# Two graph-attention layers: the first graph's lists made beside layer 0, and another order of steps in layer 1

## The chip, the core and the metric

One core of a Trainium2 chip runs the whole program. The metric is the device time of one execution in microseconds; lower is better. The core has five engines with a queue each: PE (matrix multiply, with its weight loads as PEld), DVE (vector), ACT (activation), POOL (which here also issues the gathers) and SP (which here issues most transfers). Each queue is worked off in order; engines wait for each other by semaphores.

## What is computed

There are 16 graphs of 1024 nodes with 256 features, and a dense 0/1 matrix `adj` for each. Layer 0 and layer 1 are attention layers, each followed by a residual sum and a layer norm:

```python
# layer 0, all graphs together where _bn takes its means
Wh = einsum('bnf,of->bno', x, W)
att = (Wh @ a1)[:, :, None] + (Wh @ a2)[:, None, :]
att = softmax(_bn(leaky(_bn(att, g1, b1)), g2, b2), axis=2) * adj
x = layernorm(x + elu(_bn(einsum('bij,bjo->bio', att, Wh), g3, b3)))
# layer 1, per head of 4
fts = x @ W[h]
logits = (fts @ w1[h])[:, :, None] + (fts @ w2[h])[:, None, :]
coefs = 0.5 * softmax(leaky(logits) - 1e9 * (1 - adj)) + 0.5 * softmax(adj)
x = layernorm(x + mean_h(elu(coefs @ fts + x)))
```

`_bn` in layer 0 takes the mean and variance over all graphs, so the last step of layer 0 (the factors `s3`, `t3` of the third `_bn`) can only be taken when the aggregation of all 16 graphs is finished, and layer 1 can only start from it. `adj` has few ones: layer 1 works on lists of neighbours.

## The kernel before

**Layer 0** (line 200 on). A first stage loads x, forms `wh` and casts `adj` to 16 bit; a second finds the statistics of the first two norms. The aggregation (L607 to L631) then runs over the 16 graphs. For graph b it makes 16 steps n; a step is `aggregate` (L568, four matmuls on PE), and at even n also `weights` (L525) for the graph after. After the last graph, `store` and L633 to L645 give `s3` and `t3`; L1023 makes `t31`. Outside the block that is marked as ordered by hand, the order in each engine's queue is set at build time by a scheduler that goes by the order in the text and by what is ready.

**Between the layers** (L1025 to L1135). Some hundred small DVE instructions make constants: the matrix `IW` by which h is turned, `MX`, the bit values `bits` and `add16`, `cols`, `lanes` and others. Among them are a load of one row of W, spread over all partitions (`wl`, L1120, 512 KB), and its subtraction from `W1s` (L1122).

**Lists** (class `Lists`, L1138). For each graph, lists of the columns that its groups of rows use:
- `load_rows` (L1147) loads the 16-bit adjacency in two halves of 1 MB; `words` (L1156, 32 matmuls a half) packs the bits of 25 rows into words; `worded` copies them (ACT, L1167) and sums the rest (DVE, L1171).
- `used`, then `places` (ten matmuls, L1183 to L1186) numbers the columns that are used; `placed` (L1195 to L1201) takes the number apart.
- `low`, `high`, `higher` build one-hot tables on DVE; `pick` (L1259, 64 matmuls) brings the columns into their places; `picked`, `order` (L1290) and `indices` (L1297) give `ix`, the row numbers for the gathers.

**Nodes** (class `Graph`, L1386). For each graph `load_h` (L1398) loads what layer 0 left, `exps` (ACT, L1418 and L1421) and `elu` (DVE, L1428) apply the elu in four pieces, `turn` (PE, L1434) turns it, `residual` and `beside` (DVE) add x and keep the logits, `means` and `squares` (ACT) and `spans` and `norm` take the layer norm, `factors`, `raised` and `scale` (ACT, L1481) apply it, `table` (L1508) stores the rows to memory. `halve`, `total` and `store_total` (L1530) add the sum over all rows.

**Gathers and units** (classes `Chunk` and `Unit`, L1321 and L1580). `fetch` (POOL, L1338) gathers rows by `ix`; `weigh` (DVE, and one copy on ACT at L1360) makes their weights. A graph has 16 units, two for each group of 125 + 3 rows. A unit's path: `gather` (PE, L1550, into a PSUM pair of three buffers), `invert` (DVE, L1608), `norm` (ACT, L1616, which frees the pair), `turn` and `turned` (L1622, L1632), `linear` (L1642), `add` (DVE, L1650), `exps` (L1656), `sum`, `squares`, `mean`, `span`, `power`, `close`, `store`.

**Order.** The loop at L1817 walks n from -30 to the last unit, each unit one step. The text inside the loop is the order of the queues: it is ordered by hand. `stand(part, n)` calls the side work that `side` (L1739) has filed: part 0 before the exps, 1 between the gathers on PE, 2 (loads, exps, squares, scale, fetches) and 3 (weigh). The tables `AT`, `FETCH` and `WEIGH` say at which n, counted from the graph's first unit, each step is filed. A graph's side work begins 29 units ahead, so it runs beside the two graphs before it; for the first graph there is nothing to run beside. Steps of a later graph come first in a call.

Turns and list steps share two PSUM buffers (`ps_s`).

Of the kernel before, what the change touches and what calls it, by code (L numbers as in the profile page):

```python
# [12 lines left out]
I32 = mybir.dt.int32  # L13
# [14 lines left out]
def kernel(  # L28
# [170 lines left out]

    with ExitStack() as l0:  # L200
# [17 lines left out]
        with tc.tile_pool(name="apool", bufs=1) as apool, tc.tile_pool(  # L218
# [86 lines left out]
            mts = {b: mask(mpool, b, "mt0") for b in range(min(2, B))}  # L305

# [210 lines left out]
        with tc.tile_pool(name="wk", bufs=1) as wk, tc.tile_pool(  # L517
# [47 lines left out]

            acc = {}
# [40 lines left out]
            for b in range(B):  # L607
                for n in range(NH * K):
# [416 lines left out]
    with ExitStack() as l1:  # L1025
        xpool = l1.enter_context(tc.tile_pool(name="x1pool", bufs=3))
        hpool = l1.enter_context(tc.tile_pool(name="hpool", bufs=1))
# [5 lines left out]


        TW = P + 2 * H
        IW = pk.tile([P, C, TW], F32, name="IW")
        for oc in range(C):
            nc.vector.tensor_copy(IW[:, oc, 0:P], ident)
        nc.vector.tensor_copy(IW[:, :, P:TW], WW)

        QR = (H + 1) * QB
        MX = pk.tile([P, H, QB], F32, name="MX")
        MY = pk.tile([P, H, QB], F32, name="MY")
        nc.vector.tensor_tensor(
            MX, ident[:, 0 : H * QB].rearrange("p (h q) -> p h q", h=H),
            al_bc.unsqueeze(2).to_broadcast([P, H, QB]), ALU.mult,
        )
        nc.vector.tensor_tensor(  # L1050
            MY, ident[:, H * QB : QR].unsqueeze(1).to_broadcast([P, H, QB]),
            om_bc.unsqueeze(2).to_broadcast([P, H, QB]), ALU.mult,
        )
        nc.vector.tensor_tensor(MX, MX, MY, ALU.add)

        bits = pk.tile([P, QB], F32, name="bits")
        for i in range(QB):
            nc.vector.memset(bits[:, i : i + 1], float(1 << i))  # L1060
        ibits = pk.tile([P, QB], I32, name="ibits")
        nc.vector.tensor_copy(ibits, bits)
        nc.vector.memset(bits[:, QB - 1 : QB], -float(1 << (QB - 1)))

        every = pk.tile([P, 1], I32, name="every")
        nc.vector.memset(every, (1 << QB) - 1)

        add = pk.tile([P, K, NB + 1], F32, name="add")
        pick = pk.tile([P, NB, QB], F32, name="pick")
        nc.vector.tensor_tensor(  # L1070
            pick, ident[:, 0 : NB * QB].rearrange("p (n q) -> p n q", n=NB),
            bits.unsqueeze(1).to_broadcast([P, NB, QB]), ALU.mult,
        )
        nc.vector.tensor_reduce(add[:, 0, 0:NB], pick, AX.X, ALU.add)
        nc.vector.tensor_copy(
            add[:, 1:K, 0:NB], add[:, 0, 0:NB].unsqueeze(1).to_broadcast([P, K - 1, NB])
        )
        last = pk.tile([P, K, 3], F32, name="last")
        nc.vector.tensor_tensor(
            last, ident[:, NB * QB : P].unsqueeze(1).to_broadcast([P, K, 3]),  # L1080
            bits[:, 0 : 3 * K].rearrange("p (k q) -> p k q", q=3), ALU.mult,
        )
        nc.vector.tensor_reduce(add[:, :, NB], last, AX.X, ALU.add)
        add16 = pk.tile([P, K, NB + 1], BF16, name="add16")
        nc.vector.tensor_copy(add16, add)


        cols = pk.tile([P, K, NQ], FP16, name="cols")
        jj = pk.tile([P, K, NQ], I32, tag="pi", name="jj", bufs=1)
        nc.gpsimd.iota(jj, pattern=[[P, K], [0, NQ]], base=-N, channel_multiplier=1)  # L1090
        nc.vector.tensor_copy(cols, jj)
        in8 = pk.tile([P, 8], F32, name="in8")
        nc.vector.tensor_reduce(in8, ident.rearrange("p (r q) -> p q r", q=8), AX.X, ALU.add)
        in8h = pk.tile([P, 8], FP16, name="in8h")
        nc.vector.tensor_copy(in8h, in8)
        in16 = pk.tile([P, 16], F32, name="in16")
        nc.vector.tensor_reduce(in16, ident.rearrange("p (r q) -> p r q", q=8), AX.X, ALU.add)
        in16h = pk.tile([P, 16], FP16, name="in16h")
        nc.vector.tensor_copy(in16h, in16)
        far = pk.tile([P, 24], FP16, name="far")  # L1100
        for i in range(24):
            nc.vector.memset(far[:, i : i + 1], float(2048 + P + 16 * i))


        rows = pk.tile([P, 9, 8], F32, name="rows")
        nc.vector.memset(rows, float(N))
        nc.vector.memset(rows[0:1, 0:NB, :], float(N + 1))
        nc.vector.memset(rows[0:1, 6, 0:1], float(N + 1))

        low = pk.tile([P, K, 48], FP16, name="low")  # L1110
        nc.vector.memset(low, 99.0)
        act = pk.tile([P, K + 1, NQ], BF16, name="act")
        nc.vector.memset(act, 0.0)
        lanes = pk.tile([P, 16, 8], FP16, name="lanes")
        for i in range(16):
            nc.vector.memset(lanes[:, i], float(i))


        wl = pk.tile([P, H, F], F32, tag="rw", name="wl", bufs=2)
        nc.sync.dma_start(wl, W[:, F - 1, :].partition_broadcast(P))  # L1120
        for fc in range(C):
            nc.vector.tensor_tensor(W1s[:, fc], W1s[:, fc], wl, ALU.subtract)  # L1122
# [764 lines left out]
```

The softmax here doesn't subtract the row's maximum and nothing guards it: scores larger than these inputs give would overflow.

## Time and profile before

| what | us |
|---|---|
| median of 3 runs (2366.23 to 2368.56) | 2366.42 |
| the profiled execution | 2364.92 |
| its span | 2363.2 |
| first stage and casts | 0 to 185 |
| statistics of layer 0 | 185 to 298.8 |
| aggregation of layer 0 | 298.8 to 796 |
| from there to dense work in layer 1 | 797 to 893 |
| layer 1 | 893 to the end |
| PE, DVE, ACT, POOL busy in the whole span | 2105.5, 1916.6, 1435.5, 1060.5 |

Times in the trace count from the span's start. A line of a timeline gives the start, the duration, the engine, the line of the kernel, the operation with output and inputs, the shapes, the number of instructions, and in brackets the idle time of the engine before it with what ended it. PE's clock is given as a share of full speed.

### The profile page before, as it was taken

The numbers are of one execution on the slowest core, as the hardware profiler recorded it, in microseconds if no ns is written. First come the engines' busy times: TensorE is split into PE (matmuls) and PEld (weight loads), VectorE is DVE, ScalarE is ACT, GpSimd is POOL, SyncE is SP. The second block draws the span as 40 slices with busy tenths as digits, with TensorE's granted clock in tenths as the row PEclk, the third lists the DMA queues.
The fourth block names the chain that finished last, engine by engine and source line by source line (L and its number), as shares of the span: only waits on it lengthen the run. The fifth ranks groups of instructions, "written<-read, shape, count | busy, mean of one in ns | idle before, by whom it ended". The sixth has DMA issues, their size and how long they took to land. (4 is left out here: it accounts for less than half of the span.)

```text
span 2363.2 us, 36997 instructions
## 1 busy us (share of the span) xinstructions
PE 2105.5 (89%) x12503; PEld 1647.8 (70%) x12503; DVE 1916.6 (81%) x4800; ACT 1435.5 (61%) x3028; POOL 1060.5 (45%) x1133
## 2 busy tenths in 40 slices
PE   6992479999999549899999999999999999999997
PEld 5772434444444338788888888788888788887886
DVE  3334899999999357888988989888889789898886
ACT  1122777777777226567676675675676666756665
POOL 0000100000000036776767766767767667667682
PEclk9995589999999758899999999999999999999999
DMA  8969959985553348576675685675666756756651
GB/s 258 285 191 236 263 115 244 226 206 154 155 155 93 116 147 215 160 179 174 171 196 177 157 213 162 161 206 160 181 176 172 198 162 163 210 166 164 138 149 52
DMA packets 342359, 419.75 MB, mean 178 GB/s; under 512 B 172760, under 2 KB 273168, under 8 KB 336016
## 3 DMA queue, kind: packets, MB, share of 16 engines
q1 hardware_dynamic: 285840, 256.24, 36.7%
q0 software_dynamic: 55104, 158.54, 30.4%
q10 hardware_dynamic: 1216, 2.51, 0.3%
q8 instruction: 101, 1.65, 0.3%
q14 instruction: 98, 0.80, 0.1%
HBM read 346.47 MB, written 104.29 MB: 191 GB/s over the span
## 5 line engine op out<-in xcount | busy, mean ns | idle before, releaser
L1338 POOL DMA_INDIRECT xc<-xe_dram,ix x640 | 690.7, 1079 | 184.8 <-issue 166.3
L1642 PE MATMUL pv<-W1s,sT 128*128 128x256 f32 x2048 | 504.6, 390 | 0.3 <-ACT sT L1636 0.3
L572 PE MATMUL pa<-em,wh 128*128 128x512 f32 x1024 | 451.3, 599 | 17.8 <-DVE em L536 13.4
L1642 PEld LDWEIGHTS pv<-W1s,sT 128*128 128x128 f32 x2048 | 381.6, 197 | 44.0 <-ACT sT L1636 0.7
L1622 PEld LDWEIGHTS pt<-MX,s 125*128 125x128 f32 x2560 | 355.3, 206 | 31.0 <-ACT sT L1632 9.1
L572 PEld LDWEIGHTS pa<-em,wh 128*128 128x128 f32 x1024 | 193.9, 192 | 250.4 <-issue 237.3
L1550 PE MATMUL pu<-xc,w 128*125 128x256 f32 x1280 | 365.4, 401 | 0.0
L1622 PE MATMUL pt<-MX,s 125*128 125x100 f32 x2560 | 355.6, 289 | 4.8 <-ACT sT L1632 2.9
L1656 ACT ACTIVATE m<-v,neg 128x512 f32<-128x512 f32 x256 | 184.1, 719 | 251.0 <-DVE v L1650 199.6
L1616 ACT ACTIVATE s<-pu,z 125x256 f32<-125x256 f32 x640 | 260.6, 472 | 113.3 <-DVE z L1608 63.3
L1550 PEld LDWEIGHTS pu<-xc,w 128*125 128x125 f32 x1280 | 238.6, 197 | 37.5 <-issue 6.1
L528 ACT ACTIVATE e<-eb,c,s 128x1024 f32<-128x1024 f32 x128 | 155.0, 1236 | 79.0 <-DVE sm L542 42.6
L1632 ACT COPY sT<-pt 128x500 f32<-128x500 f32 x256 | 147.1, 575 | 91.7 <-PE pt L1622 91.6
L1650 DVE TENSOR_TENSOR v<-pv,x 128x512 f32<-128x512 f32 x256 | 175.0, 683 | 8.2 <-PE pv L1642 7.9
L532 ACT ACTIVATE e<-e,v,u 128x1024 f32<-128x1024 f32 x128 | 152.3, 1229 | 22.7 <-DVE e L531 16.6
L1699 POOL TENSOR_TENSOR ors<-ors,mhalf 128x1 f32<-128x1 f32 x128 | 97.7, 764 | 149.2 <-DVE ors L1693 147.6
L536 DVE TENSOR_TENSOR em<-e,mt 128x1024 f32<-128x1024 f32 x128 | 155.6, 1218 | 3.4 <-PE pa L572 2.1
L1434 PE MATMUL pz<-IW,h 128*128 128x136 f32 x512 | 96.4, 324 | 68.1 <-DVE hi L1200 29.8
L531 DVE SCALAR_TENSOR_TENSOR e<-e 128x1024 f32<-128x1024 f32 x128 | 151.4, 1216 | 0.0
L1434 PEld LDWEIGHTS pz<-IW,h 128*128 128x128 f32 x512 | 81.7, 217 | 84.7 <-issue 46.2
L147 POOL TENSOR_TENSOR s<-var,mhalf 128x2 f32<-128x2 f32 x1 | 0.7, 710 | 311.9 <-DVE var L146 311.9
L293 DVE COPY wx<-pw 128x266 f32<-128x266 f32 x128 | 55.3, 434 | 98.3 <-PE pw L289 98.3
(320 smaller groups left out, 3558.8 us busy)
## 6 DMA issues: line engine op xcount, KB each, us to landing
x<-in_x_dram SPq DMA_DIRECT2D x32, 1024.0 KB
adj<-in_adj_dram POOLq DMA_DIRECT2D x16, 2048.0 KB
rw<-adj SPq DMA_DIRECT2D x32, 1024.0 KB
A<-u_dram SPq DMA_DIRECT2D x128, 250.0 KB
wh_dram<-wx SPq DMA_DIRECT2D x16, 1024.0 KB
wh<-wh_dram SPq DMA_DIRECT2D x16, 1024.0 KB
h_dram<-hb SPq DMA_DIRECT2D x16, 1024.0 KB
h<-h_dram SPq DMA_DIRECT2D x16, 1024.0 KB
```

Source lines behind the costliest of these rows:

```text
L528: nc.scalar.activation(e, ebs[b], AF.Identity, bias=c1[:, k, b : b + 1], scale=s1[:, k : k + 1])
L532: nc.scalar.activation(e, e, AF.Exp, bias=v2[:, k : k + 1], scale=u2[:, k : k + 1])
L536: nc.vector.tensor_tensor(em, e, mts[b][:, k, :], ALU.mult)
L572: nc.tensor.matmul(acc[b, hf, oc], wh[b][:, k, oc * P : (oc + 1) * P], ems[b, k][:, hf * HALF : (hf + 1) * HALF], start=(k == 0), stop=(k ...
L1338: nc.gpsimd.indirect_dma_start(out=self.xc[:, i, :], out_offset=None, in_=xe_dram[g.b % 2], in_offset=bass.IndirectOffsetOnAxis(ap=g.l.ix[ ...
L1434: nc.tensor.matmul(pz[:, oc, :], self.h[:, oc, k * P : (k + 1) * P], IW[:, oc, :], start=True, stop=True,)
L1550: nc.tensor.matmul(pu[0:QR, 0:F], c.w[:, k].rearrange("p h q -> p (h q)"), c.xc[:, k, 0:F], start=(i == 0), stop=(i == len(OF[q]) - 1),)
L1616: nc.scalar.mul(f.s[0:QR, i], f.pu[i][0:QR, 0:F], f.z[0:QR, i : i + 1])
L1622: nc.tensor.matmul(self.pt[:, i].rearrange("p h q -> p (h q)"), self.first.s[0:QR, i, self.hp * P : (self.hp + 1) * P], MX[0:QR].rearrange ...
L1642: nc.tensor.matmul(self.pv[:, hh, :], self.first.sT[:, fc, self.hp * HP + hh, :], W1s[:, fc, self.hp * HP + hh, :], start=(fc == 0), stop= ...
L1650: nc.vector.tensor_tensor(self.v2, self.pv, self.g.x[:, self.it].unsqueeze(1).to_broadcast([P, HP, F]), ALU.add)
L1656: nc.scalar.activation(self.m, self.v2, AF.Exp, bias=neg1, scale=1.0)
```

## The change

Four things are done.

1. The constants move from between the layers to a place in layer 0's block, right after the first stage; they lie in a pool of their own (`ek`). The pool `hpool` moves out too: it holds in turn `jj`, `wl` and `h0`, the h of graph 0.
2. The lists of graph 0 are made in the aggregation of the last graph of layer 0. Their tiles borrow buffers of layer 0 (`room`). The rows are loaded in the aggregation of the graph before, h of graph 0 at its step 4.
3. The side work of graph 0 has no lists; its x is loaded at step -29 instead of -23, and the rows of graph 1 right behind. Some numbers in the tables change.
4. In the loop over units, the steps stand in another order.

```diff
+    m1 = ExitStack()
+    ek = m1.enter_context(tc.tile_pool(name="ek", bufs=1))
+    hpool = m1.enter_context(tc.tile_pool(name="hpool", bufs=1))
...
             mts = {b: mask(mpool, b, "mt0") for b in range(min(2, B))}
+        TW = P + 2 * H
+        IW = ek.tile([P, C, TW], F32, name="IW")
...
+        wl = hpool.tile([P, H, F], F32, tag="h", name="wl")
+        nc.sync.dma_start(wl, W[:, F - 1, :].partition_broadcast(P))
+        for fc in range(C):
+            nc.vector.tensor_tensor(W1s[:, fc], W1s[:, fc], wl, ALU.subtract)
+        nc.sync.dma_start(W1s[P - 1 : P, C - 1], bias1[0:1])
...
+        h0 = hpool.tile([P, C, N], F32, tag="h", name="h_0")
...
+            def half(self, shape, dtype, name, hf):
+                if not self.room:
+                    return pk.tile(shape, dtype, tag="rw", name=f"{name}_{self.b}_{hf}", bufs=2)
+                if hf == 0:
+                    self.both = mpool.tile([P, 2 * shape[1], *shape[2:]], dtype, tag="mt", name=f"{name}_{self.b}")
+                return self.both[:, hf * shape[1] : (hf + 1) * shape[1]]
...
+        lists0 = Lists(0)
...
+            lists0.room = dict(
+                wl=(ek, "wl", 1), ix=(ek, "ix", 1), hA=(epool, "wh", 2),
+                pi=(wk, "e", 4), hi=(wk, "e", 4), hA1=(wk, "e", 4), hA2=(wk, "e", 4),
+                hm=(wk, "em", 11), V=(wk, "em", 11), E=(wk, "em", 11),
+            )
+            def make_lists(n):
+                s = lists0
+                steps = {
+                    0: [lambda: s.words(0)],
+                    1: [lambda: s.worded(0), lambda: s.words(1)],
+                    2: [lambda: s.worded(1), s.used],
+                    3: [s.places],
+                    4: [s.placed, lambda: s.high(0)],
+                    5: [lambda: s.low(0), lambda: s.low(1)],
+                    6: [lambda: s.low(2), lambda: s.low(3)],
+                    7: [lambda: s.high(1), s.higher],
+                    11: [s.pick],
+                    12: [s.picked],
+                    14: [s.order],
+                    15: [s.indices],
+                }
+                for step in steps.get(n, ()):
+                    step()
...
+                    if n == 4 and b == B - 1:
+                        nc.sync.dma_start(h0, h_dram[0])
+                    if b == B - 2 and n == 1:
+                        for hh in range(NH):
+                            lists0.load_rows(hh)
+                    if b == B - 1:
+                        make_lists(n)
...
         AT = {
-            'lh': -29, ('rw', 0): -29, ('rw', 1): -28, ('words', 0): -27, ('words', 1):
+            'lh': -29, ('rw', 0): -29, ('rw', 1): -29, ('words', 0): -28, ('words', 1):
...
-            'mean': (-17, -14), 'elu': (-26, -25, -24, -23), 'turn': (-22, -21, -19,
+            'mean': (-17, -14), 'elu': (-28, -25, -24, -23), 'turn': (-22, -21, -19,
...
         FETCH = {
-            'l': (-7,), 0: (-7, -6, -6, -6, -6), 'm': (-6, -6, -5, -5, -4), 'n': (-4,
-            -4), 1: (-4, -3, -3, -3, -3), 'o': (-2, -2), 2: (-1, -1, 0, 0, 0), 3: (1, 1,
-            1, 1, 2), 4: (2, 3, 3, 3, 3), 5: (3, 4, 4, 4, 5), 6: (5, 5, 6, 6, 7), 7: (7,
+            'l': (-7,), 0: (-7, -6, -6, -6, -6), 'm': (-6, -6, -5, -4, -4), 'n': (-4,
+            -4), 1: (-3, -3, -3, -3, -3), 'o': (-2, -2), 2: (-1, 0, 0, 0, 0), 3: (0, 1,
+            1, 1, 2), 4: (3, 3, 3, 3, 3), 5: (4, 4, 4, 4, 5), 6: (5, 5, 6, 6, 7), 7: (7,
...
         WEIGH = {
-            'l': -5, 0: -3, 'm': -2, 'n': -1, 1: 0, 'o': 0, 2: 2, 3: 4, 4: 6, 5: 8, 6:
+            'l': -5, 0: -3, 'm': -2, 'n': -1, 1: 0, 'o': 1, 2: 2, 3: 4, 4: 6, 5: 8, 6:
...
+            if g.b == 0:
+                after[AT["lh"]] += [g.load_x]
+                if B > 1:
+                    for hf in range(2):
+                        after[AT["lh"]] += [each(graphs[1].l.load_rows, hf)]
+            else:
+                after[AT["lx"]] += [g.load_x]
+            if g.b:
+                for hf in range(2):
+                    if g.b > 1:
+                        after[AT["rw", hf]] += [each(lists.load_rows, hf)]
+                    turned(AT["words", hf], lists.words, lists.worded, hf)
...
             for n in range(-EARLY, len(units) + 12):
+                do(n - 6, "add")
                 do(n - 9, "power")
-                do(n - 6, "add")
                 stand(0, n)
                 do(n - 6, "exps")
                 do(n - 3, "turn", "turned")
+                stand(2, n)
+                do(n - 7, "mean")
+                do(n - 8, "span")
+                do(n - 10, "close")
+                do(n - 5, "linear")
                 do(n - 1, "invert")
+                do(n - 11, "store")
                 do(n - 1, "norm")
-                stand(2, n)
-                do(n - 10, "close")
-                do(n - 11, "store")
-                do(n - 5, "linear")
                 if 0 <= n < len(units):
                     units[n].gather(0)
                 stand(1, n)
-                if 0 <= n < len(units):
-                    units[n].gather(1)
-                do(n - 7, "mean")
-                do(n - 8, "span")
                 stand(3, n)
                 do(n - 6, "sum")
                 do(n - 7, "squares")
+                if 0 <= n < len(units):
+                    units[n].gather(1)
```

In the queues this order means: on ACT a unit's `norm` stands behind part 2 of the side work and behind `close`; on DVE `mean` and `span` stand ahead of `invert`; on PE, POOL and SP the order of these steps is the same.

More of the change, by code (lines that the diff above doesn't have):

```diff
@@ L1050 @@
[L1050 to L1077, printed above, removed]
@@ L1098 @@
[L1098 to L1110, printed above, removed]
@@ L1750, in side @@
             after[AT["lh"]] += [g.load_h]
[L1751 to L1762 removed]
+            if g.b == 0:
[3 more added lines that the diff above has]
+                        after[AT["lh"]] += [each(graphs[1].l.load_rows, hf)]
+            else:
+                after[AT["lx"]] += [g.load_x]
[4 more added lines that the diff above has]
+                    turned(AT["words", hf], lists.words, lists.worded, hf)
+                early[AT["used"]] += [lists.used]
+                turned(AT["places"], lists.places, lists.placed)
+                for part in range(4):
+                    early[AT["low"][part]] += [each(lists.low, part)]
+                for part in range(2):
+                    early[AT["high"][part]] += [each(lists.high, part)]
+                early[AT["higher"]] += [lists.higher]
+                turned(AT["pick"], lists.pick, lists.picked)
+                turned(AT["order"], lists.order, lists.indices)
             for n in range(2 * C):
```

434 lines of the change are left out of this document (226 added, 208 removed).

## Prediction

> **What bounds the kernel now.** I read the page's slices first, then the busy time by stage, then the timelines of the passage from layer 0 to layer 1 and of one ordinary graph, then the waits of the steady stretch. (The page's chain of the last work only names the very end and is of no use here.) By stage, with the columns PE, PEld, DVE, ACT, POOL busy, clock, DMA share, GB/s:
>
> ```profile
> 770.00:797.00 27.00, 26.22 (x79) 12.79 (x78) 4.53 (x16) 4.00 (x10) 0.00 (x0) 1.00 0.18 74
> 797.00:893.00 96.00, 37.64 (x296) 28.61 (x297) 55.39 (x255) 28.00 (x66) 24.54 (x25) 0.55 0.49 150
> 893.00:2206.00 1313.00, 1244.32 (x8186) 1095.19 (x8186) 1134.88 (x3252) 859.29 (x2190) 916.33 (x947) 0.94 0.67 178
> ```
>
> In the last aggregation (770 to 797) PE is full and DVE has 22.5 us free. Then 96 us pass in which no engine is full: a chain of dependent steps. From 893 on PE is 95% busy and DVE 86%. The passage, one line each from the timelines of ACT, PE, DVE and SP:
>
> ```profile
> 798.60 0.18 ACT L594 ACTIVATION_READ_ACCUMULATOR dist<-hb,mn 128x1 f32 x1
> 812.49 0.30 ACT L1167 CAST fw<-pc 128x160 int32<-128x160 f32 x1 [13.70 <-PE pc L1156]
> ...
> 838.22 6.03 PE L1259 MATMUL po<-hA,B 128*128 128x64 f16 x64 [2.50 <-DVE fs L1451]
> ...
> 844.29 0.56 DVE L1269 TENSOR_TENSOR ptt<-po,in 128x384 f32<-128x384 f32 x1 [5.59 <-PE po L1259]
> ...
> 854.76 0.37 SPq L1508 DMA_DIRECT2D xe_dram<-x  x1
> ```
>
> Layer 0 is finished when L1023 ends at 801.8. The first exp of graph 0 needs only that and h, yet it stands behind fw on ACT, so behind the words, the constants and the load of wl: 812.7. Later `spans` (L1468) stands on DVE behind `picked` until 847.3, though its squares were done at 841.3. The node table of graph 0 is stored at 854.76, 53.0 us after 801.8; the gathers start 10.1 us later.
>
> **Part 1, lists of graph 0 and constants leave the passage: -24.9.** I rebuild it from t = 0 at 801.8, every duration from the rows of that stretch. ACT: four exp pairs, 1.55 each as at 812.7 to 819.0, so elu is done at 5.5 for the third piece and 7.1 for the fourth. PE: the eight turns need the third piece for k below 4; at the half clock of this stretch (0.50 at 815 to 820) one takes 1.1, so 5.6 to 14.4. x no longer holds residual: its load moves from step -23 to -29, and its 8.2 us (814.1 to 822.3) start, even if queued behind the last store of h, before t = 0. Residual and fs of the eighth end at 15.0, its four squares (2.5) at 17.9, spans and the power on POOL (1.9 as at 847.3) at 19.9.
>
> Here a **new wait** comes in. `elu` of graph 1 moved from -26 to -28, so graph 1's first exp pair stands on ACT ahead of graph 0's `raised` and `scale`, and its elu stands on DVE ahead of `norm` and `factors`. It needs h of graph 1, whose load waits for the eighth turn (as at 835.75) and takes 5.1: 19.6. The pair ends at 21.4, fw copy and elu at 22.6, factors (1.07) at 23.7, raised and scale (0.37 and 4.02) at 28.1. Table at 28.1 instead of 53.0: **24.9 saved**. Without that wait it would be about 2 more (27); if h of graph 1 takes the 8.2 that x took, 3 less (22). The two loads of rows of graph 1 (1 MB each) now precede h on SP; two took about 10 us at 844 to 854, and they have 14. Their words therefore don't wait as at 849.7. From table to the first gathers nothing of the chain is changed (halves, total, xr), so I keep the 10.1.
>
> **Part 2, the lists go where PE is full: +11.5.** Words 2 x 0.9, places 1.1, pick 5.9, order 0.3 as at 1511 and 1549: 9.2 of PE behind which the aggregation's last matmuls queue. Work on other engines is covered: list steps on DVE sum to about 15 (worded and used 1.4, placed 1.9, high 3.4, low 3.6, higher 1.9, picked 3.0 and index 0.2), against 22.5 free; `used` has two groups of four matmuls (3.4) for 1.9, `picked` three groups for 3.2. Without that cover PE would stand for what is missing, up to about 3 in all. Loads: rows at step 1 of graph 14 (740) for words at 771; h of graph 0 at step 4 of graph 15, 30 us early.
>
> To this comes a clock row from the same kind of pick in steady state:
>
> ```profile
> 1555.00:1557.00 2.00, 2.00 (x24) 1.81 (x22) 1.10 (x2) 0.00 (x0) 0.14 (x1) 0.50 0.59 122
> ```
>
> PE is busy all the 2 us, yet the clock is 0.50, and the turn after the pick takes 2.29 instead of 1.25 and the linear 2.92 instead of 1.92. So 2.0 to 2.4 more: 11.5. The Trainium skill ("TensorE: Matmul & The Clock Gate", Part 1: The HAM clock gate) ties the half rate to an idle window of some 3.4 us; read so, a busy PE would not fall, and the lists would cost 9.2. The row shows a fall without idle time, and I go by it. Bounds 9.2 to 15.
>
> **Part 3, constants and wl: 0.** They took DVE from 801.8 to 811.2, 7.6 of it busy. They are now emitted after the first stage. In 0 to 185 DVE is busy 69.6 of 185 under a PE that is full, and their inputs (ident, WW, alpha) exist early. The queues that they are moved past: wl's load and the bias row on SP ahead of or behind the two transposes (185 to 221), iota on POOL. If the order puts them in 243 to 283 instead, where DVE is full, they cost their 7.6. I take 0, the cover being six times their size.
>
> **Part 4, the new order in the steady loop: -16.8, the least certain.** A graph takes 92.8 us (pick to pick), PE idle 4 to 5 of it, at one place:
>
> ```profile
> 1517.13 0.70 PE L1434 MATMUL pz<-IW,h 128*128 128x136 f32 x4 [0.91 <-DVE hi L1200]
> 1519.51 1.02 PE L1434 MATMUL pz<-IW,h 128*128 128x136 f32 x4 [1.68 <-DVE sl L1563]
> ```
> ```profile
> PE pz L1434 <- DVE hi L1200: 24.7, 13, 3.0
> PE pz L1434 <- DVE sl L1563: 21.5, 13, 1.9
> ...
> DVE wl L1171 <- ACT fw L1167: 52.4, 13, 4.1
> ```
>
> (us, times, longest.) PE stands for a PSUM buffer that DVE frees late, and DVE itself stood 4.0 per graph for ACT's fw copy, which queued behind `scale`:
>
> ```profile
> 1569.71 4.03 ACT L1481 ACTIVATE x<-x,rs 128x256 f32<-128x256 f32 x8
> ...
> 1574.45 0.19 DVE L1171 TENSOR_REDUCE wl<-pc 128x8 f32<-128x32 f32 x1 [4.12 <-ACT fw L1167]
> ```
>
> With words a step earlier the copy stands ahead of scale. Not all 4.0 come back: the next DVE step, xs, needs scale itself. I place scale at 1570.1 (the exp pair of 1.6 is now ahead of it, while a norm of 1.07 goes behind): xs ends at 1574.9 instead of 1576.0 with an elu of 0.7 already done, so DVE is 1.8 ahead. Until the late place DVE also waits for transfers, 35.0 us in 13 graphs (xc 14.1 and 7.9, x 9.7 and 3.3) = 2.7 each, which takes part of it back; the store of xr should come some 1.5 earlier and shorten those. I take 1.2 per graph, 14 graphs: 16.8. Bounds: -2.0 (a loss, below) to 3.6 (both waits gone). Moving `mean` and `span` ahead of `invert` costs 0.13 per unit on DVE before z; the weighing of o a step later and five fetches shifted keep counts and engines, 0.
>
> **Sum.** The profiled execution took 2364.9 (span 2363.2 and 1.7 around it). 2364.9 - 24.9 + 11.5 - 16.8 = 2334.7; the median of the runs is 1.5 above that execution, so **2336**.
>
> **Rivals.**
>
> *The order gives nothing* (DVE's slack is lost to the transfers): only parts 1 and 2, 2366.4 - 13.4 = 2353. For it: DVE stood 3.3 for x at 1506 just ahead of the late place. Against: most graphs have smaller such waits.
>
> *Both waits go*: 3.6 per graph, 50 in 14, 2366.4 - 13.4 - 50 = 2303. For it: the clock after the waits also falls (turns 1.83 instead of 1.25), so removing them pays double. Against: xs.
>
> *Norm too late, slower.* Norm (L1616) frees the PSUM pair for the next gather, and now stands behind raised, scale and close: from the end of turned (1568.3) 0.4 + 4.0 + 0.6 + two products 0.8 = 5.8, with scale 0.4 to 1.3 later than that. PE reaches that gather (L1550) at 1574.16, 5.9 after turned. So PE stands 0.5 to 1.5 there, and less behind the squares of two other steps. If it is 2.0 per graph and not won back, 15 graphs give 30: 2366.4 - 13.4 + 30 = 2383. It decides from 13.4 / 15 = 0.9 per graph. Against: a PE that waits at unit 6 lets DVE catch up, and its wait at 13 shrinks by as much.
>
> *The lists don't fit*: PE stands in the last aggregation for DVE (3.5 more) and the constants fall into 243 to 283 (7.6): 2366.4 - 13.4 + 11.1 = 2364 with no gain from the order.
>
> **Chances.** Forecast 0.42, order gives nothing 0.20, both waits go 0.20, norm too late 0.13, lists don't fit 0.05. A measurement of this kernel tells 0.2% (4.7 us) from no change. Below 2361.7: 0.42 + 0.20 + 0.17 + 0.03 = 0.82; within: 0.07; slower: 0.11. The forecast's own range, from part 2's and part 4's nearer bounds, is 2322 to 2348; to leave out no more than 0.2 it must reach the second and third case: 2304 to 2363.
>
> **What would show it.** Part 1: L1508's first issue at about 801.8 + 11.5 + 28.1 = 841 on the clock of the trace, ACT's first L1418 right after L1023, no fw copy ahead of it. Part 2: the last L572 matmul ends near 808, with L1259 in between and a clock below 1.00 after it. Part 3: no DVE constants after 800 and no longer 243 to 283. Part 4: the wait of wl for fw falls from 4.0 to under 2 a graph, those of pz for hi and sl by about a third; the rival shows as PE waiting at L1550 for ACT s L1616. The forecast is wrong if pick to pick stays at 92.8, or if L1550 takes up such waits of 1 us or more a graph.

## The result and the profile after

The changed kernel takes **2378.89 us** (median of 20 runs, 2370.15 to 2389.76); the kernel before, measured beside it 20 times, takes 2369.02. The ratio is 1.0041, 95% interval 1.0029 to 1.0053: the change makes the kernel slower by 7 to 13 us, where 2336 was forecast. The profiled execution of the changed kernel is the slowest of its twenty, 2389.76 (span 2388.0), that of before one of 2364.92. So the two profiles stand 24.8 apart and the medians 9.9; what the profiles show of a stage has to be read with that in mind. Later series ran at two levels: in three of the five the kernel before takes 2509 to 2546 us instead of 2371, and every ratio below is to the kernel before in its own series.

Stages of the changed kernel (columns PE, PEld, DVE, ACT, POOL busy, clock, DMA share, GB/s), from the end of the 15th graph's aggregation on:

```profile
777.40:815.20 37.80, 37.78 (x225) 22.20 (x225) 18.09 (x51) 4.50 (x12) 0.00 (x0) 0.91 0.16 57
815.20:893.90 78.70, 34.54 (x185) 25.30 (x186) 41.14 (x145) 29.39 (x69) 30.57 (x29) 0.61 0.51 153
893.90:2233.00 1339.10, 1237.91 (x8157) 1079.99 (x8156) 1133.00 (x3224) 859.06 (x2185) 888.60 (x940) 0.94 0.66 173
```

PE has no gap while the lists are made, the chain between the layers is shorter by some 17 us, and the steady part has a little less work in a longer time: PE's share falls from 95% to 92%. The passage itself, from the timelines of PE, ACT and SP:

```profile
781.82 1.75 PE L449 MATMUL pc<-add,rw 128*128 128x6 bf16 x64
...
799.07 6.03 PE L552 MATMUL po<-hA,B 128*128 128x64 f16 x64
...
804.94 8.21 PE L888 MATMUL pa<-em,wh 128*128 128x512 f32 x12
...
820.79 0.81 ACT L1475 ACTIVATE hm<-h,t,s 128x512 f32<-128x512 f32 x1 [3.06 <-DVE t L1346]
...
838.19 0.81 ACT L1475 ACTIVATE hm<-h,t,s 128x512 f32<-128x512 f32 x1 [1.06 <-DMA h<-h_dram]
839.75 0.28 ACT L460 CAST fw<-pc 128x160 int32<-128x160 f32 x1
842.25 4.02 ACT L1538 ACTIVATE x<-x,rs 128x256 f32<-128x256 f32 x8
846.30 0.37 SPq L1565 DMA_DIRECT2D xe_dram<-x  x1
```

(L449 is now the words, L552 the pick, L888 the aggregation, L1475 the exps, L1565 the store of the node table.) The words and the pick stand inside the aggregation. The first exp of graph 0 starts at 820.79, right when `t31` is ready at 820.8, and the table's store is issued 25.5 us later; before it was 53.0. The exp at 838.19 is that of graph 1, ahead of `scale` at 842.25: the forecast's "new wait". The twelve matmuls after the pick take 8.21. The granted clock falls within the pick, with PE busy throughout (columns as above):

```profile
799.00:803.80 4.80, 4.80 (x44) 4.72 (x43) 0.00 (x0) 0.58 (x2) 0.00 (x0) 1.00 0.00 0
803.80:810.60 6.80, 6.80 (x31) 3.64 (x29) 2.94 (x5) 0.00 (x0) 0.00 (x0) 0.50 0.50 157
```

The steady part's waits, PE's and then DVE's, between 1000 and 2300 (us, times, longest):

```profile
PE pu L1607 <- ACT s L1673: 23.9, 32, 2.1
PE pp L476 <- DVE act L468: 21.6, 12, 2.2
PE pz L1491 <- DVE ors L1750: 20.7, 13, 1.7
PE pz L1491 <- DVE fs L1508: 13.6, 12, 2.2
PE pz L1491 <- DVE hi L493: 12.4, 9, 4.2
```
```profile
DVE x L1501 <- DMA x<-in_x_dram: 64.5, 13, 6.3
...
DVE wl L464 <- ACT fw L460: 16.1, 16, 1.3
...
DVE w L1428 <- DMA A<-u_dram: 13.0, 10, 3.3
```

DVE's wait for ACT's copy of the words went from 52.4 to 16.1, as forecast. In its place DVE now waits 64.5 for x (9.7 before), and PE waits 23.9 for `norm` (s, L1673), which is the rival's mark. From start to end, the two profiled executions compare like this ("loop" is from graph 1's picked product to the product 14 graphs on):

```
stretch                              before    after   difference
start to the aggregation              298.8    305.6        +6.8
aggregation to t31                    502.8    515.0       +12.2
t31 to graph 1's picked product       105.2     79.4       -25.8
loop, 14 graphs                      1300.2   1333.5       +33.3
rest                                  156.2    154.5        -1.7
span                                 2363.2   2388.0       +24.8
```

If the other stretches hold in the median run too, the loop's loss there is 9.9 - (6.8 + 12.2 - 25.8 - 1.7) = 18.4 us.

### The profile page after: what moved, and what is told of

Read it like the earlier page. It is cut to its first block, busy times and chain, and to the rows that moved or that the text cites. A ratio compares the mean times of both kernels' runs of the same rounds, so it can differ in the third digit from the quotient of the medians.

```text
span 2388.0 us, 36994 instructions
## 1 busy us (share of the span) xinstructions
PE 2109.2 (88%) x12503; PEld 1638.8 (69%) x12503; DVE 1920.6 (80%) x4800; ACT 1437.3 (60%) x3028; POOL 1039.6 (44%) x1133
## 5 line engine op out<-in xcount | busy, mean ns | idle before, releaser
L1392 POOL DMA_INDIRECT xc<-xe_dram,ix x640 | 676.9, 1058 | 185.3 <-issue 158.7
L888 PE MATMUL pa<-em,wh 128*128 128x512 f32 x1024 | 454.9, 602 | 18.9 <-issue 13.4
L1607 PE MATMUL pu<-xc,w 128*125 128x256 f32 x1280 | 371.3, 403 | 25.5 <-ACT s L1673 25.4
L888 PEld LDWEIGHTS pa<-em,wh 128*128 128x128 f32 x1024 | 194.1, 193 | 251.6 <-issue 235.9
L1679 PE MATMUL pt<-MX,s 125*128 125x100 f32 x2560 | 348.6, 287 | 1.8 <-ACT sT L1689 1.8
L1673 ACT ACTIVATE s<-pu,z 125x256 f32<-125x256 f32 x640 | 259.4, 468 | 105.1 <-DVE z L1665 102.4
L1607 PEld LDWEIGHTS pu<-xc,w 128*125 128x125 f32 x1280 | 233.6, 196 | 74.0 <-ACT s L1673 39.6
L1756 POOL TENSOR_TENSOR ors<-ors,mhalf 128x1 f32<-128x1 f32 x128 | 92.5, 723 | 231.1 <-DVE z L1665 195.1
L294 PE MATMUL pw<-WX,xT 128*128 128x266 f32 x512 | 127.9, 403 | 13.3 <-ACT xT L290 9.1
```

Source lines behind the costliest of these rows:

```text
L888: nc.tensor.matmul(acc[b, hf, oc], wh[b][:, k, oc * P : (oc + 1) * P], ems[b, k][:, hf * HALF : (hf + 1) * HALF], start=(k == 0), stop=(k ...
L1392: nc.gpsimd.indirect_dma_start(out=self.xc[:, i, :], out_offset=None, in_=xe_dram[g.b % 2], in_offset=bass.IndirectOffsetOnAxis(ap=g.l.ix[ ...
L1607: nc.tensor.matmul(pu[0:QR, 0:F], c.w[:, k].rearrange("p h q -> p (h q)"), c.xc[:, k, 0:F], start=(i == 0), stop=(i == len(OF[q]) - 1),)
L1673: nc.scalar.mul(f.s[0:QR, i], f.pu[i][0:QR, 0:F], f.z[0:QR, i : i + 1])
L1679: nc.tensor.matmul(self.pt[:, i].rearrange("p h q -> p (h q)"), self.first.s[0:QR, i, self.hp * P : (self.hp + 1) * P], MX[0:QR].rearrange ...
```

## The experiments

In the loop, "AT", "FETCH" and "WEIGH" are the three tables; "order" is the text inside the loop. Every kernel is an edit of the changed one. Two theories stood at first: *norm too late* (the rival: `norm` now holds the PSUM pair that PE needs) and *the tables* (the side steps that they place collide).

### Which part costs it: series A

The edits: the loop's text as before (order); the three tables as before; both; only `invert` and `norm` put back ahead of the close.

```diff
 # e1_old_order
-                do(n - 6, "add")
                 do(n - 9, "power")
+                do(n - 6, "add")
...
+                do(n - 1, "invert")
+                do(n - 1, "norm")
                 stand(2, n)
-                do(n - 7, "mean")
-                do(n - 8, "span")
                 do(n - 10, "close")
-                do(n - 5, "linear")
-                do(n - 1, "invert")
                 do(n - 11, "store")
-                do(n - 1, "norm")
+                do(n - 5, "linear")
...
                 stand(1, n)
+                if 0 <= n < len(units):
+                    units[n].gather(1)
+                do(n - 7, "mean")
+                do(n - 8, "span")
...
-                if 0 <= n < len(units):
-                    units[n].gather(1)
```
```diff
 # e2_old_tables: the changed lines of AT, FETCH and WEIGH as before; e3_lists_alone: e1 and e2 together
-            ... ('rw', 1): -29, ('words', 0): -28, ...  'elu': (-28, -25, -24, -23)
+            ... ('rw', 1): -28, ('words', 0): -27, ...  'elu': (-26, -25, -24, -23)
```
```diff
 # e4_norm_early
+                do(n - 1, "invert")
+                do(n - 1, "norm")
                 stand(2, n)
...
-                do(n - 1, "invert")
-                do(n - 1, "norm")
```

> The changed kernel with the loop over the units in the order of before (add after power, invert and norm ahead of the side steps, linear after store, both gathers round the side's matmuls, mean and span behind them); the three tables of places stay new. From the two traces: the first stage costs about 5.6 to 7.2 us more, the passage gives 14.0 back, so the lists' move alone should stand at about 2369 - 14.0 + 7.2 = 2362, and the loop from the second graph's pick on gives the rest, about +17 us in the medians. Theory 'order' (the new order of steps makes the loss: PE waits for ACT's s, act and fs) expects 2358 to 2366. Theory 'tables' (the earlier words, first elu and rows, and the shifted fetches make it) expects no gain, 2374 to 2382.

> The changed kernel with the three tables of places (AT, FETCH, WEIGH) as before; the loop over the units stays in the new order. Theory 'order' expects 2374 to 2382, within 5 us of the changed kernel. Theory 'tables' expects about 2362 (2358 to 2366). If DVE's wait for x (64.5 us in 13 graphs) comes from the tables alone and PE's wait for s (24.7 us) from the order alone, it lies half way, near 2370.

> The changed kernel with both the old order of steps and the old tables: only the lists of graph 0, the constants and the first loads are moved. If what the loop loses comes from order and tables together, 2369 - 14.0 + 7.2 = about 2362 (2357 to 2366), pick to pick back at 92.9 us. If the move of the lists or of the constants itself slows the loop (other places of the tiles, an other start of the loop), it stays at 2370 or above.

> The changed kernel with two steps alone put back: invert and norm again ahead of the side steps (elu's exps, raised, scale) and of close. The rival of the prediction 'norm too late' expects PE's wait for ACT's s to fall from 24.7 us in the loop to about 6, and with it the time by up to 18 us, to 2361 to 2366. The theory that the late load of x is the limit (DVE waits 64.5 us for it, and PE then for act and fs) expects PE's wait to move to act and fs, and 2372 to 2380.

Measured, against 2509.5 for the kernel before: new tables with the old order 1.0054 [1.0020, 1.0089]; new order with the old tables 0.9981 [0.9944, 1.0017]; lists, constants and loads alone 0.9935 [0.9901, 0.9968]; norm early 1.0041 [1.0007, 1.0075]. The passage's part is a gain and the tables cost; norm early is not enough. But a graph took 100 to 102 us here instead of 93, so the question had to be put again.

### A second level: series B and C

```diff
 # e5_old_at: AT as before.  e6_old_fetch: FETCH and WEIGH as before.
 # after_again, f0_after: unaltered.  f1 = e4, f2 = e1, f3 = e2, run again.
 # e7_lists_wl_late: e3, and the load of wl written in the third graph's aggregation
-        nc.sync.dma_start(wl, W[:, F - 1, :].partition_broadcast(P))
...
+                    if n == 1 and b == 2:
+                        nc.sync.dma_start(wl, W[:, F - 1, :].partition_broadcast(P))
```

> The changed kernel itself, unaltered, as the measure for the three beside it. The four runs so far stood on another chip, where the kernel before takes 2509.5 us instead of 2369, so nothing says yet what the changed kernel takes there. If chips matter only by a factor, 1.0041 of before (1.003 to 1.006). If the old order and the new order are alike (ratios 1.0054 and, with norm put back, 1.0041 with the new tables), also 1.003 to 1.006.

> The changed kernel with the one table AT as before: first pair of elu's exps at -26 instead of -28, words of half 0 at -27 instead of -28, row load 1 at -28 instead of -29. Fetches, weighing place of o and order of steps stay new. Theory 'first elu' (the pair of exps and the words, two units and one unit sooner, push DVE to the residual before x has landed, and put nothing in the wait's place): 0.996 to 0.999 of before, DVE's wait for x back to 10 to 20 us in the loop. Theory 'fetch' (the moved gathers share the queues with x and with the rows): no change against the changed kernel, 1.003 to 1.006.

> The changed kernel with FETCH and WEIGH as before (gathers of chunks 1, 2, 3, 4, 5 and m at their old units, o weighed at 0 instead of 1), AT and the order of steps stay new. Theory 'fetch': 0.996 to 0.999 of before. Theory 'first elu': 1.003 to 1.006, and DVE still waits about 5 us a graph for x.

> Only the move of the lists, the constants and the first loads (old order, old tables: 0.9935 of before on the other chip), and besides the load of W's last row and its subtraction from W1s put from the first stage into the third graph's aggregation (load at step 1, subtraction at step 9). The first stage then loses the 5.6 us that DVE and PE wait there for that load: 0.991 of before, that is 5 to 6 us under the lists alone, if DVE has room for two instructions of 1.23 us in the aggregation. If DVE's wait in the first stage is not on the path (the masks wait for something else), no difference from 0.9935.

Against 2536.9: the changed kernel itself 1.0329 [1.0260, 1.0398]; AT back 1.0309 [1.0249, 1.0368]; FETCH and WEIGH back 1.0072 [1.0037, 1.0107]; lists with wl written late 0.9946 [0.9918, 0.9973]. So at this level the same change costs 3.3%, and 2.6 of the 3.3 go with two tables that, in the forecast, cost nothing.

> The changed kernel itself, again as the measure for the three beside it: the eight runs so far stood on two other chips, and the changed kernel takes 1.0041 of before where the result was measured (before 2369 us) and 1.0329 on the second of the two (before 2537 us). 1.003 to 1.006 if this chip is like the first, 1.026 to 1.040 if it is like the other.

> The changed kernel with invert and norm put back ahead of the side steps and of close, nothing else. Theory 'norm too late' (the prediction's rival): at least half of what separates the changed kernel from the lists alone (0.993 to 0.995 on the other two chips) is won back, that is 1.000 or below where the changed kernel takes 1.004, and below 1.015 where it takes 1.033; PE waits for ACT's s under 8 us in the loop. Theory 'gathers' (the moved fetches): within 0.3% of the changed kernel.

> The changed kernel with the whole loop over the units in the old order, all three tables new. Theory 'norm too late' and theory 'order': as with norm alone put back, or lower. Theory 'gathers': within 0.3% of the changed kernel. If order and fetches only cost together (a fetch placed for the new order in the old one and the other way round), between the two.

> The changed kernel with all three tables as before and the new order of steps. Theory 'gathers': 0.993 to 0.999 of before. Theory 'norm too late': 1.000 to 1.004 at least, with PE's wait for s still at 20 us in the loop.

Against 2545.7: 1.0301 [1.0237, 1.0365], 0.9967 [0.9934, 1.0000], 0.9977 [0.9942, 1.0013] and 0.9986 [0.9948, 1.0024]. Here putting back norm, or the order, or the tables each takes away the whole 3%: late norm and new tables cost only together. The loss sits between the `add` of unit 11 and that of unit 12 (11.19 us in the changed kernel, 5.96 with norm early, 5.95 with the old order), where PE waits for ACT. Its waits for sT between 1000 and 2200, changed kernel first, then norm early:

```profile
PE pt L1679 <- ACT sT L1689: 47.0, 25, 4.7
```
```profile
PE pt L1679 <- ACT sT L1689: 19.1, 12, 2.9
```

At the level of the result this wait is 1.8 in all, and the same interval 5.97 in the changed kernel. Why it grows here stays open. The same two kernels do not keep their ratios from series A to C (e1 1.0054, f2 0.9977; e4 1.0041, f1 0.9967). A ratio at this level says little about the other, so the cause was sought again at the level of the result.

### At the level of the result: series D and E

The kernel before takes 2371.5 in both.

```diff
 # g0_o_at_0                      # g1_x_early
-  1: 0, 'o': 1, 2: 2,            -  'lx': -23,
+  1: 0, 'o': 0, 2: 2,            +  'lx': -24,
 # g2_norm_early_wl_late: e4, and wl written late as in e7.   g3_lists_wl_late: e7 again
 # h0_order_alone: g3 with the new order.   h1_fetch_alone: g3 with the new FETCH:
-   'm': (-6, -6, -5, -5, -4), 1: (-4, -3, ...), 2: (-1, -1, 0, ...), 3: (1, 1, ...), 4: (2, 3, ...), 5: (3, 4, ...)
+   'm': (-6, -6, -5, -4, -4), 1: (-3, -3, ...), 2: (-1, 0, 0, ...),  3: (0, 1, ...), 4: (3, 3, ...), 5: (4, 4, ...)
```

> The changed kernel with chunk o weighed at unit 0 again instead of unit 1; the gathers of FETCH stay moved, order and AT stay new. On the chips where before takes 2509 to 2546 us the changed kernel loses 5.2 us a graph between the second operands of units 11 and 12 (11.2 us there instead of 6.0 with norm early), which is where o is weighed now. Theory 'weighing of o': 0.997 to 1.003 there, that interval back at 6 us. Theory 'gathers': 1.025 to 1.035, the interval stays at 11. Where before takes 2369 us (changed kernel 1.0041) the first expects 1.000 to 1.004, the second no change.

> The changed kernel with the load of x one unit sooner (-24 instead of -23). In the changed kernel's trace DVE waits 5 us a graph for x, and from that wait to the next second operand the graph loses 3.9 us against before. Theory 'x late', on a chip like the first: that wait under 1 us, 1.3 to 2.4 us a graph won, 0.988 to 0.996 of the changed kernel, 0.992 to 1.000 of before. On the chips of the twelve runs so far DVE did not wait for x (under 1 us), so there it expects no change, 1.025 to 1.035. If x only takes the queue from the table's last store, the first gather comes later and it is slower than the changed kernel.

> The changed kernel with invert and norm early, and the last row of W loaded and subtracted in the third graph's aggregation instead of the first stage. Expected from the two single edits: 0.9967 (norm early) less 5.6 us (0.0022) is 0.9945 on the slower chips. On a chip like the first, theory 'norm too late': 1.0041 less 1 to 1.8 us a graph (15 to 25 us) less 5.6 us, 0.991 to 0.996; theory 'x late': 1.0041 less 5.6 us, 1.001 to 1.003.

> The lists, constants and first loads alone (old order, old tables), with W's last row loaded in the third graph's aggregation: 0.9946 of before in its first run. 0.992 to 0.997 again on a slower chip; on a chip like the first 2369 - 14.0 + 1.6 = about 2357, 0.993 to 0.997. If it stands at 1.000 or above there, the move of the lists costs in the loop what it wins in the passage.

Measured: o weighed as before 1.0034 [1.0020, 1.0048]; x loaded a unit earlier 1.0050 [1.0030, 1.0071]; norm early 1.0027 [1.0015, 1.0040]; lists alone 0.9937 [0.9920, 0.9953], 2355.98 us. None of the first three is apart from the changed kernel's 1.0041. Two of them show a wait that leaves without taking time along. The waits are those between 960 and 2200, where the changed kernel has 23.5 for s and 64.5 for x. With norm early (first fence) PE's wait for s is down to 0.2. With x a unit earlier (second fence) DVE's wait for x does not appear, and a wait of the same size for the rows of A stands in its place:

```profile
PE pu L1609 <- ACT s L1675: 0.2, 1, 0.2
...
DVE x L1503 <- DMA x<-in_x_dram: 26.7, 11, 4.5
```
```profile
DVE w L1428 <- DMA A<-u_dram: 61.9, 13, 6.7
```

So at this level late norm is at most a small part of the loss, and to ask for x earlier only moves the wait from x to A's rows. That pointed to the other transfers of the stretch, and so to FETCH.

> The kernel with lists, constants and first loads moved and W's last row loaded late (0.9937 of before, 2356.0 us), and the new order of steps alone on top of it; all tables old. On a chip like the first the order and the tables together cost 18 us (changed kernel 1.0041 less 5.6 us, against 0.9937). Theory 'gathers' (the moved fetches share the transfers' busy stretch with x and the rows of A): 0.992 to 0.996, graph after graph 92.9 to 93.4 us. Theory 'order': 1.000 to 1.003, 94.3 us or more a graph. On the slower chips (before 2509 us or more), where order alone stood at 0.9986 with the early load: 0.994 to 1.000.

> The same base, and the new FETCH alone on top of it (gathers of chunks 1, 2, m, 4, 5 one unit later in five places, one of chunk 3 a unit sooner); order, AT and WEIGH old. Theory 'gathers': 1.000 to 1.003 on a chip like the first, 94.3 us or more a graph, DVE's wait for x or for the rows of A over 25 us in the loop. Theory 'order': 0.992 to 0.996. If order and fetches cost only together, as on the slower chips, both runs stand at 0.992 to 0.997.

Measured: order alone 0.9927 [0.9908, 0.9946], 2352.0 us; FETCH alone 0.9993 [0.9978, 1.0007], 2369.6. Both stand on the lists' 0.9937. FETCH alone came out just under the 1.000 to 1.003 that its theory had named. **The new FETCH (five gathers a unit later, one a unit earlier) costs 0.0056, 13 us (the intervals taken together: 8 to 18); the order gives 0.0010, 2 us (not to be told from nothing).** What FETCH changes in POOL's queue can be seen in the traces. POOL's timeline around the pick of one graph, with the gathers and the `power` of a unit, first for the lists alone (the picked product is at 1362.4), then with the new FETCH (1366.0), then the changed kernel (1376.4):

```profile
1357.74 1.39 POOL L1394 DMA_INDIRECT xc<-xe_dram,ix  x1 [0.30 <-issue]
1359.43 1.01 POOL L1394 DMA_INDIRECT xc<-xe_dram,ix  x1 [0.30 <-issue]
1360.74 0.95 POOL L1394 DMA_INDIRECT xc<-xe_dram,ix  x1 [0.30 <-issue]
1365.83 0.95 POOL L1758 TENSOR_TENSOR ors<-ors,mhalf 128x1 f32<-128x1 f32 x1 [4.14 <-DVE ors L1752]
```
```profile
1361.35 1.39 POOL L1394 DMA_INDIRECT xc<-xe_dram,ix  x1 [0.30 <-issue]
1363.04 1.01 POOL L1394 DMA_INDIRECT xc<-xe_dram,ix  x1 [0.30 <-issue]
1369.41 0.95 POOL L1758 TENSOR_TENSOR ors<-ors,mhalf 128x1 f32<-128x1 f32 x1 [5.36 <-DVE ors L1752]
```
```profile
1371.40 1.39 POOL L1392 DMA_INDIRECT xc<-xe_dram,ix  x1 [0.30 <-issue]
1379.67 1.08 POOL L1756 TENSOR_TENSOR ors<-ors,mhalf 128x1 f32<-128x1 f32 x1 [6.88 <-DVE z L1665]
```

The `power` comes 3.3 to 3.4 us after the picked product in all three: it waits for DVE, and POOL's queue is in order, so no gather is issued until then. In the first kernel the last gather ahead of it is issued 1.7 us before the picked product, in the second 3.0, in the third 5.0. From the first to the second, one gather has gone behind this wait: the first of chunk 5, filed at unit 4 instead of 3. (Of the other four that moved later, those of m and 2 go behind the `power` of another unit, those of 1 and 4 behind none.) POOL stands idle before this `power` for 4.2, 5.5 and 6.8 us a graph on the mean. Some 30 us after the pick the x of the next graph is loaded, with A's rows near it. Means over graphs 4 to 14:

```
                                        before   lists   + order  + FETCH   changed
gathers issued from x's load to its use    6.1     6.3       7.1      7.9      10.3
that stretch, us                          11.9    11.9      11.9     13.6      16.4
gathered KB, 30 to 42 us after the pick   1129    1067      1194     1161      1397
other transfers there, KB                 2076    2059      2034     1894      1670
```

x is the same 1 MB each time. With FETCH and in the changed kernel x comes later, and the gathers move more bytes beside it and the other transfers fewer. But the gathers alone do not explain it: with the order alone they move more than with FETCH alone (1194 against 1161 KB), and x is no later than with the lists; and a longer stretch holds more gathers by its length. The Trainium skill ("DMA: Bandwidth & Descriptors", Queues, rings and completion order) says that a DMA engine takes its queues in turn, a packet from each. The columns for FETCH and the changed kernel would fit a load that shares its engines with gathers in this way, the one for the order does not, and the page has no price for it. What goes with x's delay on DVE and PE, in the lists alone and then with the new FETCH (960 to 2200):

```profile
POOL ors L1758 <- DVE ors L1752: 117.1, 54, 5.2
...
DVE x L1503 <- DMA x<-in_x_dram: 8.9, 8, 2.1
...
PE pp L472 <- DVE act L464: 2.9, 3, 1.4
```
```profile
POOL ors L1758 <- DVE ors L1752: 143.1, 35, 7.2
...
DVE x L1503 <- DMA x<-in_x_dram: 28.1, 12, 5.2
PE pp L472 <- DVE act L464: 12.2, 8, 2.4
```

That FETCH costs the 13 us is shown by the runs, and that DVE then waits longer for x by the traces. By what path the moved gathers delay x is not shown: the six were moved only together, and no run moved the `power` out of their way.

**What is left.** Lists 0.9937, order -0.0010 and FETCH +0.0056 make 0.9983; the changed kernel is at 1.0041. The 0.0058 between, 14 us with an uncertainty of some 7, belongs to the new AT, with o's place (g0 puts at most a few us there), and to what it costs together with the other two. In the trace it has the rest of the wait for x (26.7 with norm early, 64.5 in the changed kernel) and a slower passage: some 1.5 us more to the table. AT was not tried alone, and its share stays open. At the other level AT's return gained nothing (1.0309 against 1.0329), so the parts do not simply add.

## Why the prediction was wrong, point by point

**Part 1 (-24.9) was right**, and so was its base: the table followed `t31` by 25.5 (28.1 forecast), picked product to `t31` shortened by 25.8, and the store at 846.3 is the 841 of the forecast with part 3's loss of 6.8 on top, less 1.5. The "new wait" is there (838.19), and is worth some 1.5: with the old AT the table comes 23.9 to 24.2 after `t31`; about 2 was said.

**Part 2 (+11.5) was right**: 12.2. PE was never without work, 64 narrow matmuls of the pick took 6.03, and then the clock fell to 0.50 at 803.8 for 6.8 us. The twelve matmuls that followed would have taken 5.2 at 0.43 each, and took 8.21: 3.0 lost to the clock, 2.0 to 2.4 forecast. The choice of the row against the rule was right: the Trainium skill ("TensorE: Matmul & The Clock Gate", Part 1: The HAM clock gate) ties the half rate to an idle window, and PE's records here show none (37.78 us busy of 37.80).

**Part 3 ("I take 0") was wrong by 6.8.** The aggregation starts at 305.6 instead of 298.8. The part of it that the profile names is wl. In the changed kernel, SP's and DVE's timeline:

```profile
62.20 3.63 SPq L398 DMA_DIRECT2D wl<-in_L_gnn_W_dram  x1
...
72.77 1.23 DVE L400 TENSOR_TENSOR W1s<-W1s,wl 128x1024 f32<-128x1024 f32 x1 [7.06 <-DMA wl<-in_L_gnn_W_dram]
```

DVE stands 7.06 for it in the first stage, with the copies of PE's results behind it: the scheduler put the load at 62, not behind the first stage where the forecast saw it, and the question was not how much DVE time is free but what stands behind a DVE instruction that waits. The instructions that both kernels have stand 1.2 earlier than before just ahead of this wait and 5.6 later just behind it, and these 5.6 stay until the masks on SP behind the first stage (before, then changed):

```profile
185.36 35.94 SPq L141 DMA_TRANSPOSE mt<-adj  x2
```
```profile
190.93 35.38 SPq L141 DMA_TRANSPOSE mt<-adj  x2
```

The last 1.2 of the 6.8 come between 185 and 252, and what makes them is open. To write the load in the third aggregation did not move it (e7 and g3, the lines of g3):

```profile
61.82 4.01 SPq L930 DMA_DIRECT2D wl<-in_L_gnn_W_dram  x1
...
72.79 1.23 DVE L933 TENSOR_TENSOR W1s<-W1s,wl 128x1024 f32<-128x1024 f32 x1 [7.34 <-DMA wl<-in_L_gnn_W_dram]
```

So the 6.8 is measured, and the trace puts 5.6 of it at the wait for wl; no run took the wait away, as "wl late" left the load where it was. With it, parts 1 to 3 give -25.8 + 12.2 + 6.8 = -6.8 up to graph 1's product. g3 comes to -10.5 there, and gains 15.0 in the whole; parts 1 to 3 were forecast at -13.4 for the whole.

**Part 4 (-16.8) is the step that failed.** For the order and the tables together -16.8 was forecast; from the lists alone to the changed kernel it is +24.6 (0.0104): 13 from FETCH, -2 from the order (not to be told from nothing), and 14 that stay open. Two sentences of part 4 carry it. The first: "the weighing of o a step later and five fetches shifted keep counts and engines, 0." For o the runs show nothing else (1.0034 beside 1.0041). For the fetches it is 13 us: counts and engines stayed the same, but the places in POOL's queue did not, and x came 1.7 us later. The forecast had itself read a wait of DVE for transfers of 2.7 a graph up to that very place and taken it as something that would eat a part of the gain; it did not ask what the moved gathers would do to it. The second: of the 4.0 for ACT's copy, 1.2 were expected to come through. The wait went from 52.4 to 16.1, and it was AT that moved it (the order alone leaves 52.5, FETCH alone 52.8), but the time did not come with it. The order alone, 960 to 2200:

```profile
DVE wl L460 <- ACT fw L456: 52.5, 13, 4.1
...
DVE x L1503 <- DMA x<-in_x_dram: 16.5, 9, 2.7
```

The time from one unit's `add` to the next, mean of graphs 2 to 13 of the two profiled executions, shows the gain and the return side by side:

```
                        before   changed
units 15 and 0           13.16     11.57     -1.6
units 3 to 6             21.16     24.35     +3.2
all 16                   92.99     95.09     +2.1
```

The 1.2 per graph was had, even exceeded, at the pick, where it was expected; 3.2 was given back three to six units on, where the residual and the weights wait for x and A. PE's waits tell the same: those for sl (21.5) are gone and those for hi halved (24.7 to 12.4), as the forecast would have it, and ors, act and s stand in their place.

**The rivals.** *The order gives nothing* (2353) has the size of the order right: with old tables it runs in 2352.0. *Norm too late* (2383) names a time near the measured one, but for another reason. Its mark is there, PE waits 23.9 for s, over 1 us a graph, which the forecast had named as a mark of being wrong, and its time is not: with norm early the wait is 0.2 and the ratio 1.0027 beside 1.0041, some 3 us with intervals that overlap. The forecast said so itself ("a PE that waits at unit 6 lets DVE catch up"). At the other level, though, the late norm and the new tables do together make up the 3%. *The lists don't fit* (2364) did not happen in the last aggregation; its other half, constants that cost 7.6 of DVE's time in 243 to 283, did not either; a loss of about that size came from the constants' block in another way, as the wait for wl in the first stage.

**A version that beats both kernels**: the lists moved and the new order, with the old tables (h0), 2352.0 us, 0.9927 of before; without the order (g3) 0.9937.

## What to carry to other kernels

An edit that only shifts work within a queue isn't free because counts and engines are the same: ask which waiting instruction it goes behind and which transfers it comes to stand beside, and run it alone before it is put at 0. A named wait that goes away without time going with it (norm early, x earlier) can mean that something else is late next; the place to test is the table that moved, by putting it back alone. Where a scheduler orders the queue at build time, the place in the text is no place in the queue: read the issue in the trace before you credit the move.

## What the runs showed of the hardware that was not expected

The same kernel has two levels of time in different series: before 2371, and 2509 to 2546. With the lists alone a graph of layer 1 takes 100.7 and 102.1 us at the second level (series A and B) and 93.1 at the first (D). Layer 0's aggregation is the same, 508 to 509.5 in the kernels with the moved lists at both levels. One thing that differs in layer 1 is the copy of the words on ACT, which in such an execution (the lists alone, series A) starts late after its matmuls:

```profile
1265.44 0.94 PE L449 MATMUL pc<-add,rw 128*128 128x6 bf16 x32
...
1273.53 0.30 ACT L460 CAST fw<-pc 128x160 int32<-128x160 f32 x1 [7.86 <-remote]
```

That is 7.1 us after the words' end. In series D, for the lists alone again, the copy that is not behind `scale` follows in 0.6, and the same words in layer 0's aggregation of either execution in 0.04 to 0.34. No record names what it waits for; PE runs at half clock for 13 to 21 us a graph there, and 9 to 11 at the level of the result. The expectations above speak of chips, but the record has the same number, 6, for the chip of series A and of series E, which ran at different levels. What sets the level stays open, and a change that is a wash at one level (norm early) is worth 3% at the other.
